# Two of seven subtractions of the softmax maximum moved from VectorE to GpSimd, in a two-layer perceiver kernel

## The chip, the cores and the metric

The kernel runs on one core of one Trainium2 chip. The metric is the device time of one execution, in microseconds (us); the median of three runs is compared. The engines are named as the profile names them: PE is TensorE (PEld its weight loads), DVE is VectorE, ACT is ScalarE, POOL is GpSimd, and SP is the engine whose queue issues the DMAs.

## The reference, cut to what matters

Eight batches of 64 query rows (512 wide) pass through two layers. The part that the change touches is the first cross-attention, over a context of 1601 rows:

```python
q = (query @ Wq + bq).reshape(B, L, NKV, G, HDIM)      # 8 x 64 rows, 8 kv heads x 4 query heads, 128 wide
k_, v_ = jnp.split(kv @ Wkv + bkv, 2, axis=-1)         # from the context, 1601 rows
scores = jnp.einsum('blkgd,bmkd->bkglm', q, k) * scale
attn = jax.nn.softmax(scores, axis=-1)
o = jnp.einsum('bkglm,bmkd->blkgd', attn, v)
return o @ Wo + bo
```

After it come, for each batch, a state-space block (a scan over 64 positions), a ternary linear layer, a second cross-attention without weights over the same context, a causal self-attention and a gated feed-forward of octonion-ternary weights, each with a layer norm ahead of it and added to its input.

## The kernel before

**Units.** The first attention is cut into 64 units, one for each of 8 batches and 8 kv heads. A unit has 256 columns (4 query heads by 64 rows). Its scores are computed transposed, with the context rows on the partitions: 1601 rows make 13 tiles, held as six pairs of 128x512 (two tiles of 256 columns side by side) and one last piece of 65x256. These seven pieces are called 0 to 6 here. A loop (`x_all`) walks the units in six stages each; in the stages of one unit it also finishes the unit before:

- `x_k` and `x_v` project keys and values into PSUM (L363, L334); ACT and DVE move them to SBUF (L108, L109, L337).
- `x_s` computes the scores in PSUM (L385); ACT copies each piece to an SBUF tile S (L388), and DVE folds it into a running maximum mx (L392, L390, L395). Both free the PSUM buffer, one of four that keys, values, scores and the output projection share.
- `x_max` (one unit later) transposes mx (L403) and reduces it on DVE to the negated maximum of each column (L405). `x_spread` spreads these over all partitions with a matmul (L412), into a half of the PSUM tile m_ps, which has one buffer.
- `x_exp` takes one piece: DVE adds the spread negated maximum to S in place (L426, reading S from SBUF and m_ps from PSUM), ACT takes the exponential in place (L427), and POOL adds the pieces up: L429 for pieces 0 and 1, L452 for 2 to 5, L446 for piece 6, and L448 folds the halves into sl.
- `x_av` multiplies the pieces with the values (L464), and `x_o` sums sl over the partitions on PE (L472), takes the reciprocal on ACT and DVE and scales the output. `x_wo` is the output projection (L521).

The last unit runs with a flag, `flush`, that puts its sums on DVE.

**What runs beside it.** While the units of later batches run, the chain of the other blocks runs for each finished pair of batches as a generator that is advanced by the progress of the attention. Its instructions carry the line L65 (a wrapper). In its state-space block POOL forms the input of the scan (`a<-bc,lv`), ACT the decay (`a<-lv,c_A_log`), DVE scans (`TENSOR_TENSOR_SCAN a<-a,a`), POOL or DVE multiplies (`a<-a,bc`), and DVE reduces (`TENSOR_REDUCE a<-a`). A preparation of weights (splits, ternary weights) runs in the same way until about a third of the time, and splits `b<-b,b` on POOL. For every new batch the context is split into a high and a low part, on ACT and POOL (L105, L106, tiles cxb and cxt). What is left of the chain of the last pair follows the attention, from about 2410 us on.

**What sets the order.** A scheduler arranges the instructions of every engine before the run, from the order in which the program lists them and from when it expects their inputs; the instructions of the side chain are marked to be kept in program order. On the chip every engine runs its queue in order, and waits where an input is not there.

The pieces that each stage takes through `x_exp`, and those that `x_av` takes (13 single tiles):

```python
AVPLAN = ((), (), (0, 1, 2, 3), (4, 5, 6, 7), (8, 9, 10, 11), (12,))
EXPLAN = ((0,), (1, 2), (3,), (4, 5), (6,), ())
```

Of the kernel before, what the change touches and what calls it, by code (L numbers as in the profile page):

```python
# [11 lines left out]
ALU = mybir.AluOpType  # L12
# [4 lines left out]
P = 128  # L17
# [61 lines left out]
class Kernel:  # L79
# [336 lines left out]
    def x_exp(self, b, i, n):  # L416

        nc = self.nc
        ps = self.mm[(b, i)][0]
        S = self.S[(b, i)]  # L420
        if n == 0:
            self.ss[(b, i)] = self.sb("ss", [P, 2, 256], pool=self.xp, bufs=1)
        ss = self.ss[(b, i)]
        r, w = (P, 2) if n < 6 else (TAIL, 1)
        sv = S[n][:r, :w]
        nc.vector.tensor_tensor(sv, sv, ps[:r, 1:2].to_broadcast([r, w, 256]), ALU.add)  # L426
        nc.scalar.activation(sv, sv, AF.Exp, scale=ISC)  # L427
        if n == 1:
            nc.gpsimd.tensor_tensor(ss, S[0], S[1], ALU.add)  # L429
        elif n > 3 and self.flush:  # L430

            if n == 5:
                t = self.fs = self.sb("rw", [P, 256], pool=self.xp, bufs=1)
                nc.vector.tensor_tensor(t, S[4][:, 0], S[4][:, 1], ALU.add)
                for k in range(2):
                    nc.vector.tensor_tensor(t, t, S[5][:, k], ALU.add)
            elif n == 6:
                t = self.fs
                nc.vector.tensor_tensor(t[:r], t[:r], sv[:, 0], ALU.add)
                l = self.sb("sl", [P, 256], pool=self.xp, bufs=1)  # L440
                nc.vector.tensor_tensor(l, ss[:, 0], ss[:, 1], ALU.add)
                nc.vector.tensor_tensor(l, l, t, ALU.add)
                self.l[(b, i)] = l
                self.mm.pop((b, i))
        elif n == 6:
            nc.gpsimd.tensor_tensor(ss[:r, 0], ss[:r, 0], sv[:, 0], ALU.add)  # L446
            l = self.sb("sl", [P, 256], pool=self.xp, bufs=1)
            nc.gpsimd.tensor_tensor(l, ss[:, 0], ss[:, 1], ALU.add)  # L448
            self.l[(b, i)] = l
            self.mm.pop((b, i))  # L450
        elif n > 1:
            nc.gpsimd.tensor_tensor(ss, ss, S[n], ALU.add)  # L452
# [847 lines left out]
    def run(self):  # L1300
# [21 lines left out]
        def start(gen, now, cost, end):  # L1322
            env = {k: getattr(self, k) for k in ENV}
            if not self.tail:
                env["nc"] = Side(self, PINNED)
            side.append({"gen": gen, "cost": cost, "got": 0.0, "t0": now, "end": end, "env": env})

        def advance(now):
            base = {k: getattr(self, k, None) for k in ENV}
            for c in list(side):  # L1330
                self.setup(**c["env"])
                goal = c["cost"] * min(1.0, (now - c["t0"]) / max(c["end"] - c["t0"], 1e-9))
                if now >= c["end"]:
                    goal = 1e9
                while c["got"] < goal:
                    try:
                        c["got"] += next(c["gen"])
                    except StopIteration:
                        if PRINT_COST:
                            print("side", c["got"])  # L1340
                        side.remove(c)
                        break
            self.setup(**base)

        gi, now, xdone = 0, 0.0, 0.0
        for cost, fin in self.x_all(list(range(B))):
            xdone += cost
            if not self.flush:
                advance(xdone / X_COST)
            if fin == 0:  # L1350
# [3 lines left out]
                self.ca = actx.enter_context(tc.tile_pool(name="ca", bufs=2, side="right"))  # L1354
                start(self.prep(), xdone / X_COST, PREP_COST, PREP_END)
            if fin is not None and gi < len(groups) and groups[gi][-1] == fin:
                g = groups[gi]
                now = xdone / X_COST
                last = gi == len(groups) - 1
# [24 lines left out]
REST = {"w2":8,"b4":3}  # L1384
OTB = 1
SPV, HV = 2, 1
X_COST = 236.0
PREP_COST = 168.0
PRINT_COST = False
# [110 lines left out]
```

## Time and profile before

| what | value |
|---|---|
| median of 3 runs | 2729.16 us (2728.2 to 2729.43) |
| the profiled execution | 2721.08 us |
| its span, first to last instruction | 2719.3 us |
| mean granted TensorE clock | 0.977 |
| L426 on DVE, 448 instructions | 257.5 us busy |
| L452, L429, L446, L448 on POOL | 356.6, 84.0, 54.2, 52.8 us busy |
| L427 on ACT, 448 instructions | 247.6 us busy |
| DVE scans (L65, 96 instructions) | 153.9 us busy, 1603 ns in the mean |

The profile is one execution. "Busy" is the time in which an engine ran an instruction, not counting waits. Rows of instructions give a line, an engine, an operation, the tiles written and read, the shape and the number, then busy time and mean duration. A wait is given as who waited for whom, with the total, the number of times and the longest. A timeline row gives the start, the duration, the engine, the line, the operation and in brackets the idle time before it and what ended that.

### The profile page before, as it was taken

The page shows a single profiled execution, that of the slowest core. Times are in us where ns is not written, and L with a number is a line of the kernel's source. Part 1 is how long each engine was busy: PE and PEld are TensorE (multiplying, and loading weights), DVE is VectorE, ACT ScalarE, POOL GpSimd, SP SyncE. Part 2 cuts the span into 40 slices and gives each one's busy share as a digit, 9 for nine tenths or more (in the row PEclk, how much of TensorE's full clock was granted, in tenths as well). Part 3 has the DMA queues.
Part 4 walks back from the last instruction along what each step waited for, and adds up shares of the span by engine and source line. Part 5 has one row for each costly group of instructions (what it writes and reads, how often), then busy time and mean ns, then how long its engine had stood idle before and what let it go on. Part 6 is the DMA issues. An engine that isn't in the chain of part 4 may idle for free.

```text
span 2719.3 us, 43920 instructions
## 1 busy us (share of the span) xinstructions
PE 2565.7 (94%) x16288; PEld 2273.7 (84%) x16288; DVE 1746.8 (64%) x2843; ACT 1352.6 (50%) x3128; POOL 1171.4 (43%) x1123
## 2 busy tenths in 40 slices
PE   7999999999998899999999988999999998986888
PEld 6999999889887899978988987997897898964644
DVE  4544345577688886545568689544668879457854
ACT  4444554445565554544455554544555455445543
POOL 3212434464588643422357346421249445114610
PEclk9999999999999999999999998999999999997999
DMA  9544446665665234665234443565342463476575
GB/s 308 153 141 153 138 144 228 200 204 178 214 218 188 75 121 159 211 184 174 88 109 134 152 136 106 185 206 186 116 133 80 128 187 113 148 256 201 195 264 188
DMA packets 302934, 455.59 MB, mean 168 GB/s; under 512 B 80248, under 2 KB 179576, under 8 KB 298240
## 3 DMA queue, kind: packets, MB, share of 16 engines
q1 hardware_dynamic: 302720, 452.79, 52.2%
q8 instruction: 128, 2.10, 0.3%
q14 instruction: 86, 0.70, 0.1%
HBM read 380.23 MB, written 72.48 MB: 166 GB/s over the span
## 4 chain that ended last, share of the span: by engine, by line
PE 47%; DVE 11%; DMA 4%; POOL 3%; issue 3%; ACT 2%; POOLq 0%; DVEq 0%; ACTq 0%; SPq 0%
PE v_ps L334 10%; PE k_ps L363 10%; PE o_ps L464 6%; PE s_ps L385 5%; DVE a L65 4%; PE w_ps L521 2%; PE acc L819 2%; PE acc L777 2%; PE acc L774 1%; PE acc L1092 1%; PE acc L1036 1%; POOL a L65 1%; POOL ss L452 1%; DVE acc L953 1%; PE acc L1178 1%
## 5 line engine op out<-in xcount | busy, mean ns | idle before, releaser
L363 PE MATMUL k_ps<-cxb,wk 128*128 128x384 f32 x2304 | 473.5, 348 | 36.4 <-DVE kt L109 12.6
L334 PE MATMUL v_ps<-wv,cxb 128*128 128x256 f32 x3456 | 474.1, 283 | 7.4 <-DVE mx L392 3.9
L334 PEld LDWEIGHTS v_ps<-wv,cxb 128*128 128x128 f32 x3456 | 441.8, 190 | 28.9 <-issue 13.6
L363 PEld LDWEIGHTS k_ps<-cxb,wk 128*128 128x128 f32 x2304 | 406.8, 192 | 56.3 <-DVE kt L109 14.3
L385 PE MATMUL s_ps<-q,kt 128*128 128x256 f32 (+1 forms) x2496 | 414.5, 299 | 8.6 <-DVE mx L392 7.2
L464 PE MATMUL o_ps<-S,v 128*128 128x256 f32 (+1 forms) x1664 | 413.6, 381 | 2.6 <-DVE rw L479 1.7
L388 ACT COPY S<-s_ps 128x512 f32<-128x512 f32 (+1 forms) x448 | 242.5, 554 | 252.6 <-PE s_ps L385 249.0
L385 PEld LDWEIGHTS s_ps<-q,kt 128*128 128x128 f32 (+1 forms) x2496 | 342.0, 185 | 30.3 <-DVE mx L392 8.5
L392 DVE TENSOR_TENSOR mx<-s_ps,mx 128x512 f32<-128x512 f32 x256 | 175.4, 685 | 297.5 <-ACT S L388 297.2
L452 POOL TENSOR_TENSOR ss<-ss,S 128x512 f32<-128x512 f32 x254 | 356.6, 1404 | 14.9 <-ACT S L427 0.3
L429 POOL TENSOR_TENSOR ss<-S,S 128x512 f32<-128x512 f32 x64 | 84.0, 1312 | 640.0 <-ACT S L427 639.9
L464 PEld LDWEIGHTS o_ps<-S,v 128*128 128x128 f32 (+1 forms) x1664 | 299.4, 190 | 41.6 <-issue 5.6
L426 DVE TENSOR_TENSOR S<-S,m_ps 128x512 f32<-128x512 f32 (+1 forms) x448 | 257.5, 641 | 36.2 <-PE m_ps L412 35.4
L108 ACT ACTIVATE kt<-k_ps,c_bk 128x384 fp32r<-128x384 f32 (+1 forms) x256 | 151.8, 593 | 246.2 <-PE k_ps L363 245.4
L427 ACT ACTIVATE S<-S 128x512 f32<-128x512 f32 (+1 forms) x448 | 247.6, 600 | 41.4 <-DVE S L426 41.0
L109 DVE SCALAR_TENSOR_TENSOR kt<-k_ps,c_bk,kt 128x384 fp32r<-128x384 f32 (+1 forms) x256 | 160.9, 629 | 156.2 <-ACT kt L108 155.0
L337 ACT COPY v<-v_ps 128x256 f32<-128x256 f32 (+1 forms) x416 | 152.1, 368 | 195.8 <-PE v_ps L334 192.7
L334 PE MATMUL v_ps<-wv,cxt 128*128 128x256 f32 (+1 forms) x1536 | 211.3, 286 | 5.1 <-DVE mx L392 5.1
L334 PEld LDWEIGHTS v_ps<-wv,cxt 128*128 128x128 f32 (+1 forms) x1536 | 194.6, 176 | 17.3 <-issue 5.9
L363 PE MATMUL k_ps<-cxt,wk 128*128 128x450 f32 x768 | 179.3, 376 | 0.0
L65 DVE TENSOR_TENSOR_SCAN a<-a,a 128x512 f32<-128x512 f32 x96 | 153.9, 1603 | 32.2 <-POOL a L65 32.0
L65 ACT ACTIVATE a<-lv,c_A_log 128x128 f32<-128x128 f32 x384 | 122.8, 392 | 85.8 <-DVE a L65 84.8
(358 smaller groups left out, 3951.3 us busy)
## 6 DMA issues: line engine op xcount, KB each, us to landing
wo<-d_wo SPq DMA_DIRECT2D x96, 512.0 KB, 5.6
wk<-d_wk SPq DMA_DIRECT2D x63, 512.0 KB, 4.3
wv<-d_wv SPq DMA_DIRECT2D x31, 1024.0 KB, 5.7
cst<-in_ctxT_dram SPq DMA_DIRECT2D x96, 192.0 KB, 2.7
b<-in_ctxN_dram SPq DMA_DIRECT2D x36, 512.0 KB, 3.8
d_q<-q_t SPq DMA_DIRECT2D x32, 512.0 KB, 4.3
q<-d_q SPq DMA_DIRECT2D x64, 256.0 KB, 3.0
d_wo<-b SPq DMA_DIRECT2D x32, 512.0 KB, 2.9
```

The costliest lines, as they stand in the source:

```text
L65: return lambda *a, **k: self.tc.keep_in_program_order(f(*a, **k))
L109: eng.scalar_tensor_tensor(lo, src, bias, hi.bitcast(FP), ALU.add, ALU.subtract)
L334: nc.tensor.matmul(ps[:r], lhsT=cx[:, a, c, o : o + r], rhs=w[:, m, c, :], start=k == 0, stop=k == 11)
L337: nc.scalar.copy(vt[:r], ps[:r])
L363: nc.tensor.matmul(ps[:, :wd], lhsT=w[:, a, c, :], rhs=cx[:, m, c, :], start=k == 0, stop=k == 11)
L385: nc.tensor.matmul(sp[:r, gi, :], lhsT=kt[:, a, o : o + r], rhs=q[:, m, :], start=k == 0, stop=k == 2)
L388: nc.scalar.copy(s[:r, :n], sp[:r, :n])
L392: nc.vector.tensor_tensor(mx, sp, S[0] if len(S) == 1 else mx, ALU.max)
L426: nc.vector.tensor_tensor(sv, sv, ps[:r, 1:2].to_broadcast([r, w, 256]), ALU.add)
L427: nc.scalar.activation(sv, sv, AF.Exp, scale=ISC)
L452: nc.gpsimd.tensor_tensor(ss, ss, S[n], ALU.add)
L464: nc.tensor.matmul(ps[:, 0], lhsT=self.v[(b, j, t)][:r, hc : hc + P], rhs=S[t // 2][:r, t % 2], start=t == 0, stop=t == NT - 1)
```

## The change

In all units but the last, the subtraction of pieces 2 and 5 moves from DVE to POOL. POOL reads the spread maximum from a copy in SBUF, ms (128x256, one buffer), which ACT makes once a unit, ahead of piece 2. The exponential of both pieces stays on ACT and comes after POOL's addition. The other five pieces of a unit stay as they were.

```diff
         sv = S[n][:r, :w]
-        nc.vector.tensor_tensor(sv, sv, ps[:r, 1:2].to_broadcast([r, w, 256]), ALU.add)
+        if n in MPOOL and not self.flush:
+
+            if n == MPOOL[0]:
+                self.ms = self.sb("ms", [P, 1, 256], pool=self.xp, bufs=1)
+                nc.scalar.copy(self.ms, ps[:, 1:2])
+            nc.gpsimd.tensor_tensor(sv, sv, self.ms[:r].to_broadcast([r, w, 256]), ALU.add)
+        else:
+            nc.vector.tensor_tensor(sv, sv, ps[:r, 1:2].to_broadcast([r, w, 256]), ALU.add)
         nc.scalar.activation(sv, sv, AF.Exp, scale=ISC)
...
+MPOOL = (2, 5)
```

## The prediction

> **What bounds the kernel now.** I read the page's busy shares first, then busy time by stretch, then who waited for whom inside the worst stretch, then the instructions around its longest stall.
>
> ```profile
> PE 2565.7 (94%) x16288; PEld 2273.7 (84%) x16288; DVE 1746.8 (64%) x2843; ACT 1352.6 (50%) x3128; POOL 1171.4 (43%) x1123
> ```
>
> TensorE sets the end on average. The average hides stages, so the same by stretch (columns: stretch and length, then busy time of PE, PEld, DVE, ACT and POOL with their instructions, then clock and DMA):
>
> ```profile
> 740.00:900.00 160.00, 141.89 (x915) 134.56 (x915) 138.22 (x160) 95.05 (x229) 131.79 (x120) 0.96 0.58 192
> ...
> 1590.00:1690.00 100.00, 83.41 (x484) 76.36 (x484) 87.23 (x116) 50.97 (x139) 53.91 (x59) 0.90 0.38 121
> 1690.00:1790.00 100.00, 100.00 (x662) 94.83 (x661) 56.85 (x98) 48.44 (x113) 45.69 (x38) 1.00 0.61 198
> 2070.00:2110.00 40.00, 37.00 (x270) 32.56 (x270) 36.56 (x50) 24.11 (x61) 33.71 (x34) 1.00 0.34 102
> ```
>
> From 1690 to 1790 PE never idles, and no saving on another engine is worth anything there. It idles in the stretches where the state-space block of an earlier group runs beside the attention: 18.1 us from 740 to 900, 16.6 from 1590 to 1690, 3.0 from 2070 to 2110. DVE is 86 to 91% busy in all three, but POOL is 82 and 84% busy in the first and last and 54% in the second. PE's waits in the first:
>
> ```profile
> PEld k_ps L363 <- DVE kt L109: 7.9, 2, 5.4
> PE k_ps L363 <- DVE kt L109: 7.4, 2, 5.1
> ...
> PE v_ps L334 <- DVE mx L392: 5.3, 4, 2.4
> ```
>
> PE waits for DVE instructions that free PSUM (L109, L392). DVE runs its queue in order, so they are late when what stands ahead of them is late. What that is, the timeline at the longest stall shows:
>
> ```profile
> 844.61 1.28 POOL L65 TENSOR_TENSOR b<-b,b 128x512 fp32r<-128x512 f32 x1
> 844.69 2.28 DVE L65 TENSOR_TENSOR_SCAN a<-a,a 128x512 f32<-128x512 f32 x1 [1.89 <-POOL a L65]
> 845.85 2.18 POOL L452 TENSOR_TENSOR ss<-ss,S 128x512 f32<-128x512 f32 x1
> ...
> 851.08 0.73 POOL L446 TENSOR_TENSOR ss<-ss,S 65x256 f32<-65x256 f32 x1
> 851.15 6.59 DVE L65 TENSOR_TENSOR_SCAN a<-a,a 128x512 f32<-128x512 f32 x1
> 851.78 2.95 POOL L106 TENSOR_TENSOR cxb<-cst,cxb 128x384 fp32r<-128x384 f32 x3
> 854.69 0.72 POOL L448 TENSOR_TENSOR sl<-ss 128x256 f32<-128x256 f32 x1
> 855.38 1.28 POOL L65 TENSOR_TENSOR b<-b,b 128x512 fp32r<-128x512 f32 x1
> ```
>
> Two things to see. The scan at 844.69 waited 1.89 us for POOL's queue. And a scan that takes 1.22 us alone took 6.59 while POOL ran six instructions without a gap: the two engines hold each other up.
>
> **The change, part by part.** 63 of the 64 units change; the last runs with the flush flag.
>
> Removed from DVE: 126 of the 448 subtractions of L426. The page has the operation by duration:
>
> ```profile
> L426 DVE TENSOR_TENSOR S<-S,m_ps x448: 402/680/690, 86.0 to 2407.4; 128x512 f32<-128x512 f32 x128, 65x256 f32<-65x256 f32 x22
> ...
> L452 POOL TENSOR_TENSOR ss<-ss,S x254: 1255/1292/2363, 90.0 to 2408.0; 128x512 f32<-128x512 f32 x127
> ```
>
> (minimum/median/maximum ns). That is 126 x 0.68 = 86 us, 1.36 a unit. Its maximum is 690: it reads one operand from PSUM and is never lengthened by POOL.
>
> Added to POOL: 126 additions of two SBUF operands, 128x512, the form of L452: 1.29 us alone, 1.40 in the mean (the page's section 5), 2.36 at most. That is 163 to 177 us on 1171, or 2.8 us a unit. The Trainium skill, GPSIMD Engine Reference, section Engine selection, says to put a two-input elementwise operation on VectorE since GpSimd takes about twice as long; the rows here say 1.9 times.
>
> What the added work does to DVE: in the three wider stretches (580 to 940, 1440 to 1690, 2070 to 2320) I compared each DVE instruction with the fast tenth of its own group; they ran 120 us over among 489 POOL instructions, 0.25 us for each. For one added POOL operation the bounds are about nothing (the first ones run beside DVE's remaining subtractions, which are immune) and 1.29 us (a whole POOL operation waited out); I take 0.25, the mean of its neighbours, so 0.5 a unit. The Trainium skill, SBUF — State Buffer, section Who interferes with whom, states that a DVE instruction with two SBUF inputs and a GpSimd instruction that reads SBUF block each other fully, while one with a single SBUF input does not contend. The immune 690 ns of L426 and the 6.59 us scan agree. By that rule the change swaps work that cannot contend for work that does, at up to 1.29 us each: 2.6 a unit, more than the 1.36 saved.
>
> Added to ACT: 63 copies of 128x256 out of PSUM, nearest row L337 at 0.37 us: 23 us on an engine that is 50% busy. Cover: ACT's idle time; uncovered, 0.37 a unit. m_ps has one buffer and is now freed earlier; ms has one buffer, needed again a unit (some 30 us) later: nothing.
>
> The new wait: the exponentials of pieces 2 and 5 wait on ACT for POOL. In the build's order POOL has both additions right behind the first sum (L429) in 60 of 63 units, and ACT has those two exponentials last, behind the one of piece 6. From the end of exponential 1, POOL needs 3 x 1.3 = 3.9 us for sum and additions; ACT's seven ended 2.4 to 4.5 us after it in most units, so ACT waits little when POOL starts at once. It does so where
>
> ```profile
> POOL ss L429 <- ACT S L427: 639.9, 56, 38.2
> ```
>
> POOL stood idle for the exponential in 56 of 64 units. In four tight ones L429 began 3.0, 2.4, 1.9 and 2.3 us late (units whose L426 start at 754.8, 788.5, 1449.8, 2069.9). There ACT would stand still for up to that, with S copies (L388) and kt (L108) behind it, which free PSUM for PE: 9.5 us at most; I take a third, 3, since ACT has idle time elsewhere in each unit.
>
> Who else waits on the later sums: L472 on PE reads sl. It came 2 us after sl at the least (units at 788.5, 897.1, 2028.8), otherwise 4 to 23, so a sum 2.8 us later touches PE in few units.
>
> The sum, by place:
> - POOL-tight units (754.8, 788.5, 828.4, 865.0, 1449.8, 2069.9, 2106.6): 7 x 2.8 = 19.7 us later on POOL, and DVE's scans wait for POOL. Half passes on, since POOL idles 18% there and DVE gets 1.36 back: +10.
> - DVE-tight units with a POOL that idles (1586.4, 1637.0, 1685.1, 2223.5, 2257.7, 2303.0): 6 x (1.36 - 0.5) = -5.
> - ACT's waits: +3.
> - The other 50 units: PE full or nearly, 0. The tail after 2410 holds none of these instructions.
>
> Together +8 us. The profiled execution took 2721.08 (span 2719.3), so 2729 for it; the median of the runs is 8.1 above it, so **2737** at the median.
>
> **The rivals.** *Faster: DVE's relief reaches PE.* Every long PE stall of these stretches ends on a DVE instruction, which speaks for it; in 30 units of the new order a maximum (L392) now runs between the subtractions, where before it did in one, so a PSUM buffer is freed up to 2 us sooner. 25 units lie in stretches with stalls; 25 x (1.36 - 0.5) = -21 us, from which the usual part would be -12, so 2717. It decides if POOL's additions land where POOL idles. Against it stand POOL's 82 to 84%.
>
> *No change:* gain and loss cancel, or the scans wait for other things (DMA of bc, ACT) anyway: 2729.
>
> *Much slower: bursts.* POOL's nine operations of a unit run without gaps, scans starve as at 851, and PE's clock drops after the stall (0.90 in the 1590 stretch): the 7 tight units at 2 x 2.36 = 4.7, 33 us, with ACT's 9.5 makes +42, so 2771. For it: the scan of 6.59. Against: most DVE instructions get in after one POOL operation.
>
> That the change does not do what it says is excluded: the build has 126 fewer instructions on DVE, 126 more on POOL, 63 more on ACT. But the scheduler arranges every queue anew, so a stall may move by some us either way for no reason of the change.
>
> **How the numbers follow.** Slightly slower (forecast, its own range 2732 to 2749: POOL-tight units passing on from a quarter to all of their 19.7 us) 0.37; much slower 0.15; no change 0.20; faster 0.28. A measurement of this kernel tells about 0.2% (5.4 us) from no change. The range runs from most of the relief (-15: 2714) to most of the burst (+36: 2765).
>
> **What would show it.** Right: POOL busy 1320 to 1370, DVE near 1690; more time under DVE waiting for POOL at L65; PE idle up from 740 to 900 and from 2070 to 2110, down from 1590 to 1690; some ACT exponentials waiting for POOL. Wrong: PE idle falls in all three stretches, or ACT waits for POOL in most units.

## The result, and the profile after

| | before | after |
|---|---|---|
| median of 6 runs each, taken in turn | 2728.68 us (2718.99 to 2729.54) | 2743.77 us (2740.75 to 2745.94) |
| ratio, with its 95% interval | | 1.0062 [1.0046, 1.0078] |
| profiled execution, and its span | 2721.08, 2719.3 us | 2740.75, 2738.9 us |

The change makes the kernel 15.1 us slower. The forecast was +8, to 2737. Profiled executions are single ones: the 25 runs of before that were made beside the last experiments lie between 2721.75 and 2735.94 us, so a difference of some us between two profiles alone says little.

The page's line of busy time, of after:

```profile
PE 2562.8 (94%) x16288; PEld 2267.4 (83%) x16288; DVE 1704.7 (62%) x2717; ACT 1379.3 (50%) x3191; POOL 1327.8 (48%) x1249
```

POOL did 156 us more than before (1171.4), DVE 42 less (1746.8), although the subtractions' own busy time fell by 71 (257.5 in before, 186.1 in after; it is less than 126 x 0.68 = 86 because the time in which two neighbours overlap counts once). The other 29 us came back as longer instructions on DVE.

Three wide stretches hold all the forecast's tight units. Busy time by stretch (columns as in the prediction), of before:

```profile
580.00:940.00 360.00, 331.21 (x2133) 309.92 (x2133) 284.36 (x406) 193.03 (x451) 235.92 (x224) 0.97 0.57 180
...
1440.00:1690.00 250.00, 229.78 (x1469) 214.33 (x1469) 200.43 (x285) 133.69 (x331) 129.80 (x133) 0.96 0.44 135
...
2020.00:2320.00 300.00, 283.45 (x1828) 256.72 (x1827) 242.08 (x349) 160.52 (x400) 177.14 (x173) 0.99 0.42 127
```

The same of after:

```profile
580.00:940.00 360.00, 323.51 (x2049) 298.95 (x2049) 264.38 (x372) 190.32 (x447) 257.92 (x239) 0.95 0.56 181
...
1440.00:1690.00 250.00, 227.47 (x1459) 209.50 (x1458) 191.10 (x267) 136.08 (x340) 161.55 (x154) 0.97 0.42 130
...
2020.00:2320.00 300.00, 278.38 (x1793) 252.46 (x1791) 239.04 (x328) 162.52 (x404) 195.01 (x189) 0.98 0.39 122
```

PE's idle time (length less busy) went from 28.8 to 36.5 us, from 20.2 to 22.5, and from 16.6 to 21.6. DVE is less busy in all three and PE idles more in all three: what DVE got back did not reach PE. (The windows are the same times, not the same work, since after falls behind; the unit marks below compare the same work.) Between these stretches PE is full in both kernels.

Who waited for whom over the whole execution (total us, times, longest), of after:

```profile
ACT S L434 <- DVE S L433: 76.7, 66, 5.0
DVE a L65 <- POOL a L65: 68.5, 46, 4.2
...
DVE S L433 <- ACT ms L430: 26.7, 30, 2.1
...
ACT S L434 <- POOL S L431: 12.8, 24, 1.6
```

and of before:

```profile
DVE a L65 <- POOL a L65: 58.6, 41, 3.5
```

DVE's wait for POOL's queue grew by 10 us. ACT's wait for POOL's additions is short and rare, 24 of 126. The third line was not foreseen: one of DVE's remaining subtractions waits for ACT's copy. L430 and L433 read the same PSUM tile, m_ps, and in the built program the two reads are kept apart by a dependency. The Trainium skill, PSUM — Partial Sum Buffer, section "PSUM bank collisions raise a hardware error", says that two engines must not read one bank of the same partitions at once and that software has to order them; no run here shows a collision. ACT has the copy behind the exponential of piece 1, so DVE waits for that too.

To see where the time went unit by unit, I took from both traces the moment at which PE starts a unit's sum over the partitions (`o_ps<-sl,ones`). After runs 0.5 us ahead of before at unit 18 (742 us), 22.3 behind at unit 22 (918), 14.3 behind at unit 26, 19.2 at unit 45, 33.4 at unit 53 (2089) and 29.6 at unit 63. From there to the end it takes 296.7 us, where before takes 306.6. So the attention lost 30 us and the tail, which holds none of the changed instructions, got 10 shorter. From the first mark to the last PE idles 71.5 us in before and 88.9 in after.

### The profile page after: what moved, and what is told of

Read it like the earlier page. It is cut to its first block, busy times and chain, and to the rows that moved or that the text cites. A ratio compares the mean times of both kernels' runs of the same rounds, so it can differ in the third digit from the quotient of the medians.

```text
span 2738.9 us, 43863 instructions
## 1 busy us (share of the span) xinstructions
PE 2562.8 (94%) x16288; PEld 2267.4 (83%) x16288; DVE 1704.7 (62%) x2717; ACT 1379.3 (50%) x3191; POOL 1327.8 (48%) x1249
## 4 chain that ended last, share of the span: by engine, by line
PE 66%; DVE 13%; DMA 7%; POOL 6%; issue 4%; ACT 3%; SPq 1%; POOLq 0%; DVEq 0%; ACTq 0%
PE v_ps L334 16%; PE k_ps L363 15%; PE o_ps L471 10%; PE s_ps L385 8%; DVE a L65 5%; PE acc L274 3%; PE w_ps L528 2%; PE acc L826 2%; POOL a L65 2%; PE acc L1043 2%; PE acc L1099 2%; PE acc L781 1%; PE acc L784 1%; DVE b L65 1%; DMA cst<-in_ctxT_dram 1%
## 5 line engine op out<-in xcount | busy, mean ns | idle before, releaser
L471 PE MATMUL o_ps<-S,v 128*128 128x256 f32 (+1 forms) x1664 | 415.1, 384 | 12.8 <-DVE rw L486 7.5
L459 POOL TENSOR_TENSOR ss<-ss,S 128x512 f32<-128x512 f32 x254 | 347.4, 1368 | 28.1 <-ACT S L434 17.4
L434 ACT ACTIVATE S<-S 128x512 f32<-128x512 f32 (+1 forms) x448 | 253.2, 598 | 90.9 <-DVE S L433 76.7
L433 DVE TENSOR_TENSOR S<-S,m_ps 128x512 f32<-128x512 f32 (+1 forms) x322 | 186.1, 625 | 49.3 <-ACT ms L430 26.7
L65 DVE TENSOR_TENSOR_SCAN a<-a,a 128x512 f32<-128x512 f32 x96 | 171.1, 1783 | 39.9 <-POOL a L65 39.9
L363 PE MATMUL k_ps<-cxt,wk 128*128 128x450 f32 x768 | 184.8, 379 | 5.7 <-DVE mx L392 5.7
L431 POOL TENSOR_TENSOR S<-S,ms 128x512 f32<-128x512 f32 x126 | 177.2, 1430 | 0.0
```

What stands on the lines that cost most here:

```text
L65: return lambda *a, **k: self.tc.keep_in_program_order(f(*a, **k))
L363: nc.tensor.matmul(ps[:, :wd], lhsT=w[:, a, c, :], rhs=cx[:, m, c, :], start=k == 0, stop=k == 11)
L431: nc.gpsimd.tensor_tensor(sv, sv, self.ms[:r].to_broadcast([r, w, 256]), ALU.add)
L471: nc.tensor.matmul(ps[:, 0], lhsT=self.v[(b, j, t)][:r, hc : hc + P], rhs=S[t // 2][:r, t % 2], start=t == 0, stop=t == NT - 1)
```

## The experiments

Theory A, the prediction's: POOL's added time, in the units where POOL is tight, delays DVE's and ACT's queues and through them PE. (A2, a variant: what delays DVE is that both engines read SBUF, so that only an operation that reads does harm.) Rival B: DVE's new wait for ACT's copy. Rival C: the scheduler's new order of all queues, for no reason of the work itself.

### One part at a time, each in an order of its own

e1_relief leaves the two subtractions out and puts nothing in their place:

```diff
+        if n not in MPOOL or self.flush:
+            nc.vector.tensor_tensor(sv, sv, ps[:r, 1:2].to_broadcast([r, w, 256]), ALU.add)
```

> Leaves out the subtraction of pieces 2 and 5 altogether (all units but the last): DVE is relieved of 126 x 0.68 = 86 us, GpSimd and ScalarE get nothing. Theory A (the loss of the change is GpSimd's added work, and DVE's relief is worth little): 2709 to 2724, 5 to 20 us faster than the kernel before. Theory B (the loss is DVE's new wait for ScalarE's copy of the maximum): the relief alone should be worth the same 5 to 20 us, so it doesn't tell A from B. Theory C (a new arrangement of the queues moves the time by 10 to 15 us whatever the cause): the time may lie above the kernel before although work is only taken away.

Measured: 2738.74 us against 2726.88 for before, which was run again beside each group of experiments, ratio 1.0046 [1.003, 1.0063]. With 86 us of work removed from DVE and none added anywhere, the kernel became 12 us slower. In the profiled executions the attention ends 12 us later than in before and the tail is 8 longer (314.9).

e2_load leaves DVE all seven subtractions and gives POOL four half-size additions a unit, written to an unused tile:

```diff
+        if n in MPOOL and not self.flush:
+            d = self.sb("ms", [P, 256], pool=self.xp, bufs=1)
+            for k in range(2):
+                nc.gpsimd.tensor_tensor(d, sv[:, 0], sv[:, 1], ALU.add)
```

> DVE does all seven subtractions as before; GpSimd gets four more additions of 128x256 a unit (4 x 0.73 = 2.9 us, the change added 2.8), which read the exponentials of pieces 2 and 5 into a scratch tile that nobody reads. No copy, and no exponential waits for GpSimd. Theory A: 15 to 30 us slower than the kernel before (2744 to 2759), lost between 740 and 930 and near 1450 and 2090. Theory B: within 5 us of the kernel before.

Measured: 2746.37, ratio 1.0076 [1.0057, 1.0095]. POOL's busy time rose by 192 us (1171.4 to 1363.7). By the marks above, 13.3 us came in the attention and 16.6 in the tail (profiled execution).

e3_copy makes ACT's copy at piece 2, which nobody reads, and leaves all else:

```diff
+        if n == MPOOL[0] and not self.flush:
+            self.ms = self.sb("ms", [P, 1, 256], pool=self.xp, bufs=1)
+            nc.scalar.copy(self.ms, ps[:, 1:2])
```

> ScalarE copies the spread maximum at piece 2 as in the change, nobody reads the copy, and DVE does all seven subtractions from PSUM. Theory A: within 4 us of the kernel before. Theory B: 8 to 16 us slower (2737 to 2745), with DVE waiting for the copy some 25 us in total.

Measured: 2723.92, ratio 0.9993 [0.9981, 1.0005]. DVE waits for the copy here as it does in after (29.4 us, 34 times), and the time does not move. That speaks against B, as far as a kernel in an order of its own can.

e4_late moves pieces 5 and 6 in place of 2 and 5, so that DVE has done its five subtractions before the copy and has nothing left that waits for it:

```diff
-MPOOL = (2, 5)
+MPOOL = (5, 6)
```

> The change with pieces 5 and 6 in the place of 2 and 5: DVE does its five subtractions first, then ScalarE copies, so DVE has nothing left to wait with; GpSimd gets 1.4 + 0.85 us a unit in the place of 2.8. Theory A: three quarters of the loss stay, 8 to 13 us slower than the kernel before. Theory B: the loss is gone, 0 to 15 us faster than the kernel before.

Measured: 2790.22, ratio 1.0235 [1.0211, 1.0258], four times the loss of the change, where theory A expected 8 to 13 us and B none. DVE's wait for the copy is gone from the list of waits, which speaks against B once more. Two things took its place. ACT waits for POOL's additions 53.1 us in 46 waits (12.8 in after). And DVE starves. The timeline of e4_late:

```profile
853.08 8.86 DVE L65 SCALAR_TENSOR_TENSOR lv<-lv,c_Dp,a 128x128 f32<-128x128 f32 x1
...
853.96 1.27 POOL L459 TENSOR_TENSOR ss<-ss,S 128x512 f32<-128x512 f32 x1
...
855.20 1.25 POOL L65 TENSOR_TENSOR b<-b,b 128x512 fp32r<-128x512 f32 x1
856.40 0.10 POOL L65 MEMSET a<- 128x8 f32 x1
856.46 0.45 POOL L65 TENSOR_TENSOR lv<-lv,lv 128x128 f32<-128x128 f32 x1
...
856.88 1.26 POOL L459 TENSOR_TENSOR ss<-ss,S 128x512 f32<-128x512 f32 x1
...
858.10 1.25 POOL L65 TENSOR_TENSOR a<-bc,lv 128x512 f32<-128x512 f32 x1
859.32 1.25 POOL L65 TENSOR_TENSOR b<-b,b 128x512 fp32r<-128x512 f32 x1
860.54 1.25 POOL L459 TENSOR_TENSOR ss<-ss,S 128x512 f32<-128x512 f32 x1
...
861.87 0.67 DVE L109 SCALAR_TENSOR_TENSOR kt<-k_ps,c_bk,kt 128x450 fp32r<-128x450 f32 x1
...
862.59 2.93 PE L334 MATMUL v_ps<-wv,cxb 128*128 128x256 f32 x12 [7.49 <-DVE kt L109]
```

A DVE instruction whose shortest run in the same execution is 0.33 us holds the engine for 8.86, while POOL runs eight instructions without a gap, from 853.96 on. It ends when POOL's row ends. kt stands behind it on DVE, and PE stands still for 7.49 us for kt. In this execution 21 DVE instructions (6 in before) took over 2.5 us, and DVE was busy 1795.2 us, more than before with 126 more instructions. How much of the 63 us goes by each of the two was not separated.

What follows from the four: a removal that costs 12 us says that C is real, and that such a comparison, each kernel in its own order, cannot tell terms of 5 to 15 us. The next kernels therefore keep an order fixed: every instruction is issued and arranged as in the kernel named, and only afterwards are marked instructions made narrower or wider. The order of every queue is then the same, and so are the waits that are written into it; the traces list the same instructions in the same order on DVE, ACT and POOL.

```diff
-            nc.gpsimd.tensor_tensor(sv, sv, self.ms[:r].to_broadcast([r, w, 256]), ALU.add)
+            t = nc.gpsimd.tensor_tensor(sv, sv, self.ms[:r].to_broadcast([r, w, 256]), ALU.add)
+            MARK.append(t.ins.name)
...
+def shape(ap):
+    return [list(ap[0]), [1, 8]]
...
+    edit(nc, shape)
```

### The order of after, with POOL's additions cut

f1_after_no_pool is that diff: the 126 additions are cut from 512 columns to 8.

> The changed kernel with every queue in exactly its order, but GpSimd's 126 additions cut from 512 to 8 columns once the order is fixed (so pieces 2 and 5 are hardly subtracted): GpSimd loses its 2.8 us a unit, DVE keeps its relief, the copy and all waits stay. Theory A (GpSimd's added work): the loss goes, 2710 to 2724. Theory C (the order in which the scheduler put the queues): 8 to 15 us slower than the kernel before as the changed kernel is, 2735 to 2744.

f2_after_half cuts them to 256 columns (`[1, 256]` in `shape`).

> The same with 256 of 512 columns (0.73 in the place of 1.3 us): theory A: half way between the changed kernel and the one with 8 columns, some 2730. Theory C: as the changed kernel, 2740 to 2745.

Measured, with the additions' median length and POOL's busy time from the profiles:

| kernel | one addition | POOL busy | DVE busy | time | ratio to before |
|---|---|---|---|---|---|
| f1_after_no_pool | 0.204 us | 1185.0 | 1664.3 | 2718.60 | 0.9957 [0.9938, 0.9976] |
| f2_after_half | 0.749 us | 1255.8 | 1677.2 | 2728.48 | 0.9996 [0.9982, 1.001] |
| after | 1.310 us | 1327.8 | 1704.7 | 2743.77 | 1.0062 [1.0046, 1.0078] |

In one order, POOL's added time alone is worth 25.2 us, and half of it 9.9. f1 still has the copy, DVE's wait for it (26.4 us, 30 times) and the same order, and beats before by 10 us. So the copy, DVE's relief and the order together are a gain, and the loss is POOL's added time: A. From the first mark to the last PE idles 66.8 us in f1, 22 less than in after. DVE's wait for POOL's queue, of f1:

```profile
DVE a L65 <- POOL a L65: 53.2, 35, 4.0
```

In this order the additions thus add 15 us to that wait (68.5 in after), 12.8 to ACT's, and 40.4 to DVE's busy time.

The same stretch of both timelines shows it happen (unit 22; start, length, engine, operation). Of f1_after_no_pool:

```profile
863.59 1.28 POOL L437 TENSOR_TENSOR ss<-S,S 128x512 f32<-128x512 f32 x1
...
864.83 1.50 POOL L431 TENSOR_TENSOR S<-S,ms 128x8 f32<-128x8 f32 x2
...
865.87 0.39 DVE L485 SCALAR_TENSOR_TENSOR sl<-rw,sl 128x256 f32<-128x256 f32 x1
...
866.19 0.69 DVE L65 TENSOR_TENSOR a<-a,bc 128x512 f32<-128x512 f32 x1
...
866.80 0.41 DVE L487 TENSOR_TENSOR rw<-o_ps,sl 128x256 f32<-128x256 f32 x1
...
868.03 1.89 PE L472 MATMUL o_ps<-S,v 128*128 128x256 f32 x8
```

Of after:

```profile
874.00 1.30 POOL L436 TENSOR_TENSOR ss<-S,S 128x512 f32<-128x512 f32 x1
...
875.26 3.65 POOL L431 TENSOR_TENSOR S<-S,ms 128x512 f32<-128x512 f32 x2
...
876.31 1.44 DVE L484 SCALAR_TENSOR_TENSOR sl<-rw,sl 128x256 f32<-128x256 f32 x1
...
877.67 1.78 DVE L65 TENSOR_TENSOR a<-a,bc 128x512 f32<-128x512 f32 x1
...
879.38 0.41 DVE L486 TENSOR_TENSOR rw<-o_ps,sl 128x256 f32<-128x256 f32 x1
...
879.84 1.99 PE L471 MATMUL o_ps<-S,v 128*128 128x256 f32 x8 [0.98 <-DVE rw L486]
```

From POOL's first sum to DVE's rw it is 3.2 us in f1 (866.80 - 863.59) and 5.4 in after (879.38 - 874.00). The two DVE instructions in between have both operands in SBUF and run beside POOL's additions: 1.44 in place of 0.39, and 1.78 in place of 0.69, together 2.1 us. The instruction behind them is 2.2 us late, and PE, which lost nothing there in f1, stands still 0.98 us for it. The five subtractions that DVE keeps in this unit, with one operand in PSUM, are as long in both (1.27 us for two, 1.61 for three).

By the unit marks, after falls behind f1 by 12.4 us from unit 18 to unit 22, 2.6 at unit 38, 5.4 at units 53 and 54, 5.5 at units 13 and 14, 2.5 at units 58 and 59, and by nothing in the units where PE is full. That these steps are no chance of two executions, two more profiles in the same order show (the kernels come below): g2, which has the full additions in units 18 to 22, 38, 53 and 54 but not in 13 and 14, falls behind f1 by 9.8, 6.0, 4.4 and 0.5 us in these four places; g1, which has them in 13 and 14 alone of these, by 0.6, 0.0, 0.1 and 5.1.

### The order of before, with DVE relieved or POOL loaded

f3_before_relief cuts the subtractions of pieces 2 and 5 on DVE to 8 columns, in before's order:

```diff
+        t = nc.vector.tensor_tensor(sv, sv, ps[:r, 1:2].to_broadcast([r, w, 256]), ALU.add)
+        if n in (2, 5) and not self.flush:
+            MARK.append(t.ins.name)
```

> The kernel before with every queue in exactly its order, but DVE's subtractions of pieces 2 and 5 cut from 512 to 8 columns once the order is fixed (those pieces are hardly subtracted). DVE's relief alone, without a new arrangement, about 1.1 us a unit. Theory A (relief is worth up to 0.86 us in 25 units): 5 to 20 us faster, 2708 to 2723. Theory C says the same, and that the 12 us that the first run of relief lost were its order. If DVE's relief is worth nothing even so: within 4 us of the kernel before.

Measured: 2724.94, ratio 0.9982 [0.9968, 0.9996]: 3.7 us faster, less than the 5 to 20 that theory A had expected. A cut subtraction still takes 0.15 us, so DVE lost some 67 us of work (126 x (0.68 - 0.15)), not 86. The relief by itself is worth about 4 us, and the 12 us that e1_relief lost go with its order.

f4_before_load widens POOL's own sums L429 and L452 from 512 columns to 768, in before's order (it reads the first 256 columns of each piece three times, so its sums are wrong):

```diff
+            t = nc.gpsimd.tensor_tensor(ss, ss, S[n], ALU.add)
+            MARK.append(t.ins.name)
...
+    return [list(ap[0]), [1, 768]] if ap[0][0] == 768 else [list(ap[0]), [0, 3], [1, 256]]
```

> The kernel before with every queue in exactly its order, but GpSimd's five sums of a unit (L429, L452) widened from 512 to 768 columns once the order is fixed, 5 x 0.56 = 2.8 us a unit, the load that the change adds (the sums are wrong: the third part repeats the first half of a piece). DVE keeps all its work, nothing waits for GpSimd anew. Theory A: 15 to 25 us slower, 2742 to 2752. Theory C: within 5 us of the kernel before.

Measured: 2791.84, ratio 1.0237 [1.0213, 1.026], 63 us slower for 179 us more on POOL, where theory A expected 15 to 25. Its busy line:

```profile
PE 2591.3 (93%) x16288; PEld 2290.4 (82%) x16288; DVE 1821.4 (65%) x2843; ACT 1351.5 (48%) x3128; POOL 1350.5 (48%) x1123
```

DVE's instructions are those of before in the same order, and yet it is 75 us busier: only POOL's sums differ, so these are instructions held up while POOL works. e2_load gave POOL a like amount and lost 20 us in an order that the scheduler had made for it; in an order made without it, the loss is three times as large. The order need not be the whole reason: e2's additions are shorter (0.74 us in the median against 1.84) and nobody waits for their result.

### Where in the execution the additions cost

g1_cut_tight cuts the additions, in after's order, in 19 units only (18 to 24, 37, 38, 41 to 44, 53 to 55, 58 to 60: all of the prediction's tight units and their neighbours). g2_cut_rest cuts them in the other 44.

```diff
+            if 8 * b + i in TIGHT:
+                MARK.append(t.ins.name)
```

> The changed kernel with every queue in exactly its order; GpSimd's additions are cut to 8 columns only in 19 units around the stretches where TensorE stalls (units 18 to 24, 37, 38, 41 to 44, 53 to 55, 58 to 60), and keep 512 columns in the other 44. Theory A (the loss is made where the side chain runs on DVE and GpSimd): nearly as with all of them cut, 2718 to 2724. If the loss is spread over all units: 44 of 63 of the 25 us stay, some 2736.

> The reverse: full additions in those 19 units, cut ones in the other 44, same order. Theory A: as the changed kernel, 2738 to 2745. If the loss is spread: 19 of 63 of the 25 us, some 2726.

Measured: g1 2724.32, ratio 0.9992 [0.9981, 1.0003]; g2 2736.76, ratio 1.0038 [1.0021, 1.0055]. Against before, run beside them, these are -2.5 and +10.0 us, where f1 was -10.1 and after +15.1. So the additions of the 19 units cost 18 us (15.1 + 2.5) to 20 us (10.0 + 10.1), and those of the 44 others 5 (15.1 - 10.0) to 8 (10.1 - 2.5). Both times lie a little outside what theory A expected (2718 to 2724, 2738 to 2745) and far from a loss spread over all units (2736, 2726). Units 13 and 14, which the marks show losing 5.5 us, are among the others.

### Must the added work read SBUF?

g3_memset puts two memsets of the same piece in the place of each addition; they read nothing. g4_memset_cut has the same order with the memsets cut to 8 columns.

```diff
-            nc.gpsimd.tensor_tensor(sv, sv, self.ms[:r].to_broadcast([r, w, 256]), ALU.add)
+            for _ in range(2):
+                t = nc.gpsimd.memset(sv, 0.0)
+                MARK.append(t.ins.name)
```

> In the place of each addition GpSimd sets the piece to zero twice (two memsets of 128x512, some 0.5 us each by the row of 128x1024, 2 us a unit; the pieces are zeroed, not subtracted): it occupies GpSimd's queue and ScalarE waits for it, but it reads nothing from SBUF. Its own order. To be compared with the next run, which has the same order. Theory A1 (the loss comes through the queue: work behind the additions is late): 18 us above the next run (100 of 140 us of the load that cost 25). Theory A2 (the loss comes through reads of SBUF, which hold up DVE's instructions with two SBUF operands): 0 to 4 us above the next run.

> The same program in the same order with the memsets cut to 8 columns once the order is fixed. The base for the run before it; both theories: 2712 to 2735, by its order.

Measured: g3 2728.20, ratio 1.0003 [0.9992, 1.0014]; g4 2710.89, ratio 0.9946 [0.9931, 0.9961]. A memset takes 0.526 us, cut 0.104. The difference is 17.3 us for 92.9 us of POOL's busy time (1287.4 - 1194.5). The waits for the memsets, of g3_memset:

```profile
ACT S L436 <- POOL S L432: 63.1, 76, 4.1
```

and of g4_memset_cut:

```profile
ACT S L436 <- POOL S L432: 26.0, 31, 3.3
```

DVE's busy time rose only 9.6 us from g4 to g3 (1666.9 to 1676.5), against 40.4 from f1 to after. So memsets hardly lengthen DVE's instructions, and cost as much per microsecond: here the exponentials that wait for POOL are the likelier way, with 37 us more of such waits, though that was not tried by itself. A2 falls as the only way; POOL's queue has two ways to PE.

All pairs together, the share of POOL's added busy time that reached the end:

| pair | order | added on POOL | added at the end | share | added on DVE |
|---|---|---|---|---|---|
| f1 to f2 (half the addition) | after's | 70.8 us | 9.9 us | 14% | 12.9 us |
| f1 to after | after's | 142.8 | 25.2 | 18% | 40.4 |
| g4 to g3 (memsets) | their own, the same in both | 92.9 | 17.3 | 19% | 9.6 |
| before to f4 | before's | 179.1 | 63.2 | 35% | 74.6 |
| before to e2 | each its own | 192.3 | 19.5 | 10% | 22.4 |

Not settled: how much of the change's 25 us goes by DVE's longer instructions, how much by DVE's waits for POOL and how much by ACT's; the three meet in the same units. ACT's are the smallest (12.8 us in all). Why the tail of after is 10 us shorter than that of before was not tried by itself, but it goes with the order: the three profiles in before's order (before, f3, f4) have tails of 306.4 to 307.7 us, the five in after's order (after, f1, f2, g1, g2) of 296.7 to 305.4. A kernel that computes everything and moves the additions only in the units where PE is full was not tried: it would get an order of its own, and g1, which leaves out the additions of the 19 tight units without giving DVE that work back, is only 2.5 us under before. Of the kernels here none that computes everything beats before by more than the measurement can tell.

## Why the prediction was right, and where its terms were off

**Direction, cause and place: right; the way only in part shown.** It put the loss on POOL's added time in the units where POOL is 82 to 84% busy. The fixed orders show that: 25 us from POOL's additions alone, three quarters of it in the 19 tight units, and the first large step (12.4 us, units 18 to 22) in the stretch whose timeline it quoted. It let the delay pass through DVE's scans that wait for POOL. Those waits did grow (by 15 us from f1 to after), but DVE's longer instructions are the larger sum (40 us), and which of the two carries the delay to PE is open. Of its signs, PE's idle time rose from 740 to 900 (18.1 to 19.8 us) and from 2070 to 2110 (3.0 to 4.3), as said; from 1590 to 1690 it did not fall (16.6, 16.7).

**The added work: right.** POOL busy 1327.8 (forecast 1320 to 1370), an addition 1.310 us in the median and 1.43 in the mean (forecast 1.29 and 1.40). DVE 1704.7 (forecast near 1690).

**What an added operation does to DVE: right, a little low.** 0.25 us forecast; 40.4 / 126 = 0.32 measured between f1 and after. The Trainium skill, SBUF — State Buffer, section Who interferes with whom, calls the ports that the two engines share an exclusive lock, over which a DVE instruction with two inputs in SBUF contends with a GpSimd instruction that reads SBUF and not with one that only writes. The subtractions with an operand in PSUM (at most 0.69 us in before) and the memsets (9.6 us on DVE for 92.9 on POOL) agree. Read as a wait for one POOL instruction, as the forecast's bound of 1.29 us had it, the lock falls short: the rows of e4_late show a DVE instruction held through eight (8.86 us).

**POOL-tight units: the mis-sized term.** "Half passes on: +10." By the unit marks the seven units named there (19 to 22, 38, 54, 55) fell behind f1 by 18.3 us (12.4 + 2.6 + 3.3), while their additions took 16.7 us more than in f1: all of it passed on, not half. The half rested on POOL idling 18% of those stretches. In after its idle time lies where it waits for ACT or DVE (4.72 us ahead of 870.53), and behind the additions of these seven units the next idle moment of over 0.1 us comes after 1.9 us in one and 7.8 to 28.4 in the others; what stands right behind the additions has no gap to be caught up in.

**"The other 50 units 0": wrong by some 8 us.** By the marks units 13 and 14, where PE also idles, lost 5.5 us and unit 53 lost 2.1. Units 58 and 59, of the DVE-tight ones, lost 2.5 more. Where PE is full the zero holds: from unit 22 to 37 after gains or loses less than a microsecond on f1.

**DVE's relief, -5: near in size, its place not shown.** f3_before_relief is worth 3.7 us over the whole kernel. In the six units that the forecast named, after gains 2.5 us on before from unit 41 to 44, with PE idle as long (16.6 and 16.7 us), and loses 1.8 from unit 57 to 60: a gain of 0.7 in place of 5. What PE idles more from 1440 to 1690 lies at unit 38, a POOL-tight one (2.5 us before, 4.7 after).

**ACT's waits, +3:** 12.8 us of them, 24 times, at most 1.6; what they cost at the end could not be told apart. They did not come "in most units", which would have spoken against the forecast.

**"The tail untouched": wrong.** It is 10 us shorter in after and 6 in f1 (300.5 us) than in before. Because of this f1's 10 us under before are no measure of the relief: in the profiled executions f1's attention is 3.6 us longer than before's and its tail 6.1 shorter. If the relief is worth in after's order what it is in before's, 3.7 us, some 6 of the 10 are the order's, an estimate; the forecast had named the order ("a stall may move by some us either way") and not priced it.

So +15 is +25 for POOL's additions (forecast 10 and 3) and -10 for everything else (forecast -5). Both terms were about half of what they are, and the errors offset each other in the sum: that the total came out as near as it did is in part luck. (The upper end of the forecast's own range, 2749, does not come out of its sum: 19.7 - 5 + 3 is 18, so 2747.)

## What to carry to other kernels

Judge the room on an engine in the stretch where the work will land and by what stands behind it in the queue: POOL was 43% busy on average, and two additions a unit, 2.8 us, passed on whole in the units where it was over 80% busy. Here moving work off an engine that is not the bound bought little (67 us off DVE, 4 us at the end), while added work on an engine that others wait for cost 10 to 35% of its length. The most was in an order that was not made for it (f4), but the pairs differ in more than the order. Under a scheduler, change a size with the order held fixed before you believe a term of some 10 us: e1 removed work and was 12 us slower, and in a fixed order nearly the same removal was 4 us faster.

## What the runs showed of the hardware

- A run of POOL instructions without gaps can hold one DVE instruction with two SBUF operands for the whole run: 6.59 us in before, 8.86 and 11.81 in e4_late, for instructions that take 1.22 us in the median, 0.33 at the shortest, and 0.68 to 1.34 in the other five cases of the last one. I had expected a wait of one POOL instruction.
- POOL's addition of two SBUF operands on 128 partitions took 0.204, 0.749, 1.310 and 1.842 us (medians) for 8, 256, 512 and 768 columns (the last reads 256 columns three times), so about 0.2 us and 2.2 ns a column; a memset of 512 columns took 0.526 us. Cutting POOL's work by columns is therefore a fair way to dose it.
- Memsets, which read nothing, lengthened DVE's instructions by 0.10 us per added microsecond of POOL (9.6 / 92.9), additions by 0.28 (40.4 / 142.8), and both cost 18 to 19% at the end.
